# Segment attention with batch norm: unit weights for six segments' rows replaced by gathered weights, and 24 edge products a group by 16

## The chip, the cores and the metric

The kernel runs on one core of a Trainium2 chip. The metric is the device time of one execution in microseconds. Three timed executions of the kernel before gave 340.02, 339.72 and 338.75 us; the median is 339.72 us.

The engines as the profile names them: PE multiplies matrices (PEld is its loading of weights), DVE does vector work, ACT does activations and copies, POOL issues the indirect transfers (gathers and scatters) and some small vector work, SP issues the plain transfers. Each engine takes its instructions in order.

## The reference

There are 16384 tokens of 256 numbers (`feat`), and each has a segment number 0 to 7 (`bids`). The segment numbers are not sorted.

```python
q = feat @ Wq                 # 32 columns
k = feat @ Wk                 # 32 columns
v = feat @ Wv                 # 256 columns
starts = jnp.searchsorted(bids, jnp.arange(B))
pos = jnp.arange(N) - starts[bids]
pad = lambda x: jnp.zeros((B, LMAX, x.shape[-1])).at[bids, pos].set(x)   # LMAX 3072
mask = jnp.zeros((B, LMAX), bool).at[bids, pos].set(True)
scores = where(mask[:, None, :], qp @ kp^T, -1e9)
rp = softmax(scores) @ vp
t = rp[bids, pos] @ Wt
tn = (t - t.mean(axis=0)) / sqrt(t.var(axis=0) + EPS) * gamma + beta
return feat + relu(tn)
```

Because `bids` is not sorted, `pos` can be negative or beyond LMAX, and two tokens can be written to the same place of a segment. A token whose write stands is an *owner*; a token whose place was overwritten is a *loser*, and it reads the owner's row. A token whose position lies outside of the window reads the row at the window's near end: these are the *edge rows*, two for each segment, 16 in all. The mean and the variance go over all 16384 tokens, so every row of `t` counts as often as tokens read it.

## The kernel before, in words

**Owners.** The owners of segment `e` are gathered from `feat` into up to FT = 6 tiles of 128 rows, `xs[e*6 .. e*6+5]`. `list_ahead`, `list_sums` and `list_rows` work out the list of their tokens (`idx`) on DVE and PE, and `list_rows` issues three gathers on POOL for each half. There are 8 segments, so `xs` and the result `tk` have TT = 48 tiles. The losers make up LT = 3 tiles; their list is number NB = 8, their `feat` rows are in `xl` and their result rows in `tl`.

**Attention.** The loop over `e` works on segment `e` and prepares segment `e+1`. For each of six query tiles, `step(e, u)` calls `attend` (scores are exponentials in `pa` and `pb`, the product with the values in `vs`, a reciprocal) and `scale`, which writes `tk` and, after tiles 3 and 5, stores rows to the array `t_rows` in HBM through SP's queue. Between the steps stand the projections of the next segment, the lists of the segment after the next, and small jobs from the list `work` that `slot` takes one by one: `places`, `edges`, `fill_rows`, `rows`.

**Weights of rows.** `reads_r` has a column for each of the 48 tiles: how many tokens read each owner's row directly. `places().f` works out the counts by token and stores them to `reads_of` in HBM. For segments 0 to 5 (EARLY_B = 6), `list_ahead` sets the column to 1 where there is an owner and to 0 elsewhere, with one operation on DVE; the losers of these segments are added to the sums as rows of their own. For segments 6 and 7, `gather_reads` gathers the counts with six POOL gathers of one number a partition. After segment 6 the POOL queue gathers the losers' rows of segments 0 to 5 into `tl` (three gathers).

**Sums.** `square` squares a row tile on ACT into one of four buffers `sq`; `moments` adds the row and its square, each times its weight, into `acc` (two DVE operations). `past(e)` does `n` = 0, 0, 1, 1, 2, 2, 1, 1 pairs each time that it is called in segment `e`; in the last segment it has a branch of its own that does two pairs while loser tiles stand at the head of `lag` or more than one tile is waiting. The last segment takes its tiles in the order 0, 1, 4, 5, 2, 3, and after tile 3 what is left is done. Tile 1 of the last segment goes by PE (`by_row`) instead. At the end PE adds `acc` and the edge rows over the partitions into `sums`.

**Edge rows.** `ecat` holds the 16 edge rows, repeated so that partition `p` has row `p mod 16`: a gather from `t_rows` brings those of segments 0 to 6, and products with `sel` (written by POOL) add those of segment 7. `edge_of` holds for each token the code of its edge row, or a code of none. The codes are brought to all 128 partitions by 16 transfers through `eb`, and compared with `emod` (the partition number mod 16) into `hot`, a one-hot matrix in BF16.

**Statistics to output.** From `sums` DVE makes mean, variance, scale and shift (`ss`). Then it normalizes the edge rows (`ye`) and splits their positive part into three BF16 parts `y3[0..2]` whose sum is the value in full precision. The 16 output groups are of 1024 tokens each. For group `k`, `open_group` puts PAIRS[k] of its four pairs of `feat` tiles into PSUM by a product with the identity; 24 products (2 halves `u`, 3 parts, 4 row groups `r`, 16 partitions each) add the edge row of each token that reads one; DVE adds the other pairs, ACT copies those that PE opened, and SP stores 1 MB. From `k` = 3 on, DVE also normalizes one segment's owners after each group (`normal`, `normal_more`). POOL then scatters the owners' rows and the losers' rows over the stored groups, each segment after the groups that it needs (`finish` counts them).

**Order.** Waits are put in by the program class from what each operation reads and writes; each queue works in the order written. All operations are recorded by helpers, so the profile gives the helpers' lines: products L802, transposes L807, activations L812, copies L817 (ACT) and L818 (DVE), two-input operations L821, operations with a scalar L828 and L830, three-input operations L839 and L841, reciprocal L854, plain transfers L872, gathers L877, scatters L885 and L893, group loads L1703, group stores L1928.

Of the kernel before, what the change touches and what calls it, by code (L numbers as in the profile page):

```python
# [14 lines left out]
AF = mybir.ActivationFunctionType  # L15
ALU = mybir.AluOpType
# [884 lines left out]
def fast_path(nc, feat, bids, wq, wk, wv, wt, gamma, beta, out, bad):  # L901
# [74 lines left out]
    y3 = [at(f"y3{i}", [P, D], BF16, addr(acc) + 512 * i) for i in range(3)]  # L976

    pcol, pm, emod = new("pcol", [P, 1]), new("pm", [P, 1]), new("emod", [P, 1])
    ecol, rcol = new("ecol", [P, NB]), new("rcol", [P, FT])
    cbeg, cend, n_bc = new("cbeg", [P, NL]), new("cend", [P, NL]), new("n_bc", [P, NL])  # L980
    n_1 = new("n_1", [P, NL])
# [127 lines left out]
    pg.tt(sm[:], sm[:], sc_[:], ALU.subtract, eng="POOL")  # L1109
    pg.tt(sm[:], sm[:], sa[:], ALU.add, eng="POOL")  # L1110

    EARLY_B = NB - 2

    def zero_fill(e):
        rows = xs[:, e * FT : (e + 1) * FT, :].rearrange("p t d -> p (t d)")
        pg.copy("ACT", rows, zero[:].to_broadcast([P, FT * D]))
# [32 lines left out]
    def list_ahead(e):  # L1149
        T = FT if e < NB else LT  # L1150
        pg.ts(ge[:, 0, 0 : T * P], it16[:, 0 : T * P], cbeg[:, e : e + 1], ALU.is_ge)
        pg.ts(ge[:, 1, 0 : T * P], it16[:, 0 : T * P], cend[:, e : e + 1], ALU.is_ge, -1.0, ALU.mult)
        pg.ts(pad[:, 0:T], rcol[:, 0:T], n_bc[:, e : e + 1], ALU.is_ge, float(N), ALU.mult)
        if e < NB:
            m = slice(e * FT, e * FT + T)
            pg.ts(mask[:, m], rcol[:, 0:T], n_1[:, e : e + 1], ALU.is_ge, NEG, ALU.mult)
        if e < EARLY_B:
            pg.ts(reads_r[:, m], rcol[:, 0:T], n_bc[:, e : e + 1], ALU.is_lt)

    def list_sums(e, h, ps=None):  # L1160
        ps = nb() if ps is None else ps
# [132 lines left out]
    squared = []  # L1294

    def square(e, u):
        x = sq[turn[1] % (4 if e < NB - 1 else 3)]
        turn[1] += 1
        if e == NB:
            row, w = tl[:, u, :], ones[:, 0:1]  # L1300
        else:
            n = e * FT + u
            i = n - TT + FT - 2
            row, w = tk[:, n, :], rw[:, i : i + 1] if i in (0, 1) else reads_r[:, n : n + 1]
        pg.act(x[:], row, AF.Square)
        return row, w, x

    def own_of(e):
        pg.ts(own1[:], b_f[:], float(e), ALU.is_equal)
        pg.stt(own1[:], tok[:], st_lo[:, e : e + 1], own1[:], ALU.is_ge, ALU.mult)  # L1310
# [13 lines left out]

    pg.copy("POOL", bs_f[:], bs_i[:])
    def moments():
        row, w, s = squared.pop(0)
        pg.stt(acc[:, 0, :], row, w, acc[:, 0, :], ALU.mult, ALU.add)
        pg.stt(acc[:, 1, :], s[:], w, acc[:, 1, :], ALU.mult, ALU.add)

    cast_bids()
    pg.ts(own0[:], b_f[:], 0.0, ALU.is_equal, pm[:], ALU.mult)
# [118 lines left out]
    def edges():  # L1451
        def a():
            pg.ts(parts_i[:], pci[:], 2 * NB - 1, ALU.bitwise_and)
            pg.copy("DVE", emod[:], parts_i[:])
            pg.ts(g16[:], irow[0:1, 0:NG], float(GT * P), ALU.mult)
            pg.ts(at_g[:], g16[:], float(GT * P), ALU.add)
            lo = st_lo[0:1, :].unsqueeze(2).to_broadcast([1, NB, NG])
            hi = st_hi[0:1, :].unsqueeze(2).to_broadcast([1, NB, NG])
            pg.tt(over_g[:], hi, g16[:].unsqueeze(1).to_broadcast([1, NB, NG]), ALU.is_gt)
            pg.tt(over_h[:], lo, at_g[:].unsqueeze(1).to_broadcast([1, NB, NG]), ALU.is_lt)  # L1460
            pg.tt(over_g[:], over_g[:], over_h[:], ALU.mult)
            pg.red(need[:], over_g[:].rearrange("x e g -> x g e"), ALU.max)
            pg.scan(nth[:], ones[0:1, 0:NG], need[:])
# [171 lines left out]
    def fill_rows():  # L1635
        def zeros(x):
            f = x[:].rearrange("p t d -> p (t d)")
            pg.copy("ACT", f, zero[:].to_broadcast([P, f.shape[1]]))

        def a():  # L1640
            zeros(acc)
            pg.set("DVE", ridl[:], NB * FW)
            pg.set("DVE", reads_r[:, EARLY_B * FT : TT], 0.0)
            pg.tr32(gb[:].rearrange("p s i -> p (s i)"), graw[:].rearrange("p s i -> p (s i)"))

        def b():
# [10 lines left out]
    def by_row(w, row, x):  # L1657
        pg.mm(sums[:, 0:D], w[:], row, start=False, stop=False)
        pg.mm(sums[:, D : 2 * D], w[:], x[:], start=False, stop=False)

    work.extend(places())
# [12 lines left out]
    def past(e):  # L1674
        n = (0, 0, 1, 1, 2, 2, 1, 1)[e]
        if past_e[0] != e:
            past_e[:] = [e, 0]
        e_ = (e - 5) * FT + past_e[1]
        past_e[1] += 1
        if 0 <= e_ < NB:  # L1680
            load("DVE", ("td", e_), arm[0:1, e_ : e_ + 1], 2)
        if e == NB - 1:
            for _ in range(2 if lag and lag[0][0] == NB or len(lag) > 1 else 1):
                if squared:
                    moments()
                if lag:
                    squared.append(square(*lag.pop(0)))
            return
        for _ in range(n):
            if squared:  # L1690
                moments()
        for _ in range(n):
            if lag:
                squared.append(square(*lag.pop(0)))
# [12 lines left out]
    for e in range(NB):  # L1707
# [18 lines left out]
        if last:  # L1726
            for u in (0, 1, 4, 5, 2, 3):
                step(e, u)
                if u == 0:
                    for g in range(EARLY):  # L1730
                        load_group(g)
                    scores(e, 1, range(4))
                    late[0]()
                    late[1]()
                if u == 1:
                    scores(e, 1, range(4, 6))
                    late[2]()
                    pg.gather(ecat[:, 0, :], t_rows[0 : (NB - 1) * FW, :], eidx[:], (NB - 1) * FW)
                if u == 4:
                    late[3]()  # L1740
                if u == 0:
                    lag[:0] = [(NB, t) for t in range(LT)]
                if u == 5:
                    first = square(e, 1)
                    for g in range(EARLY, MID):
                        load_group(g)
                if u == 1:
                    pg.act(row_sum[:], ones[:], AF.Identity, scale=reads_r[:, e * FT + 1 : e * FT + 2])
                if u == 3:
                    any_ = hot[0 : 2 * NB, 0:2, :, :].rearrange("p k u x -> p (k u x)")  # L1750
                    pg.mm(sums[:], none[0 : 2 * NB, :], any_, start=True, stop=False)
                    by_row(row_sum, first[0], first[2])
                if u == 3:
                    while lag or squared:
                        if lag and len(squared) < 2:
                            squared.append(square(*lag.pop(0)))
                        else:
                            moments()
                else:
                    past(e)  # L1760
                if u == 2:
                    b_e = ps_s[0]
                    for u_ in (0, 4, 5, 1):
                        pg.mm(
                            b_e[:, 0:D], sel[:, u_, :], tk[:, e * FT + u_, :], start=(u_ == 0), stop=(u_ == 1),
                            pred=over4(e, u_),
                        )
                    pg.tt(ecat[:, 0, :], ecat[:, 0, :], b_e[:, 0:D], ALU.add)
                    pg.act(ecat[:, 1, :], ecat[:, 0, :], AF.Square)
        else:  # L1770
# [18 lines left out]
            step(e, 2, lambda: project(n, 1))  # L1789
            if busy:  # L1790
                list_part(e + 2, 1)
            past(e)
            slot(1 if busy else 2)
            if e + 3 < NB:
# [6 lines left out]
                own_of(e + 3)  # L1801
            if not busy:
                slot(2)
            if EARLY_B <= e + 1:
                gather_reads(e + 1)
            if e == 3:
                losers()[0]()
# [17 lines left out]
        pg.end_region()  # L1825
        if e == NB - 2:
            slot(99)
            for t in range(LT):
                pg.gather(tl[:, t, :], t_rows[0 : EARLY_B * FW, :], ridl[:, t : t + 1], EARLY_B * FW)
            pg.set("POOL", none[:], 0.0)  # L1830
    for e_ in range(NB + 1):
        load("POOL", ("g", e_), upto[0:1, e_ : e_ + 1], NG, 1)
# [50 lines left out]
    open_group(1)  # L1883
    pg.tt(ye[:], ecat[:, 0, :], scale, ALU.mult)
    pg.tt(ye[:], ye[:], shift, ALU.add)
    pg.ts(y3[0][:], ye[:], 0.0, ALU.max)
    pg.stt(yf[:], ye[:], 0.0, y3[0][:], ALU.max, ALU.subtract)
    pg.copy("DVE", y3[1][:], yf[:])
    pg.tt(y3[2][:], yf[:], y3[1][:], ALU.subtract)
    pg.tt(bad[:], b[:, 0:1], cnt_f[:, 0:1], ALU.add)  # L1890

    def normal(m, T, y=tk, x=xs):
# [40 lines left out]
    for k in range(NG):  # L1933
# [120 lines left out]
```

## Time and profile before

| what | value |
| --- | --- |
| median of three executions | 339.72 us |
| the profiled execution's own time | 340.02 us |
| its span (first to last instruction) | 335.6 us |
| outside of the span | 4.4 us |
| mean granted clock of PE | 0.865 |
| busy: PE, PEld, DVE, ACT, POOL | 258.8, 169.9, 238.0, 151.4, 135.4 us |
| `xs` gathers on POOL | 48, 1063 ns each |
| `reads_r` gathers on POOL | 12, 999 ns in the median |
| edge products `ps<-y,hot` | 384, in 16 groups of 24 |
| accumulations `acc` with `reads_r` | 45 and 45, 476 and 483 ns each |
| HBM read and written | 26.27 and 28.74 MB |

How to read it: in rows of single instructions or groups, the first number is the start in us from the beginning of the span, the second the duration in us (of several instructions of a kind, from the first to the last), then come engine, line, operation, the tile written and those read, and how many. In square brackets stands how long the engine was idle before it and what ended that. "remote" and "another core or an unknown queue" are put where the profile shows no instruction that ended at the time of the signal. In rows by windows, the columns are the stretch and its length, the busy time of PE, PEld, DVE, ACT and POOL with their counts, the granted clock of PE, the busy share of the DMA engines, and GB/s.

The execution has four stretches: lists, weights and first segment up to about 70 us; the middle segments up to about 217 us; the last segment with the statistics up to about 248 us; the output from there to the end.

### The profile page before, as it was taken

The numbers are of one execution on the slowest core, as the hardware profiler recorded it, in microseconds if no ns is written. First come the engines' busy times: TensorE is split into PE (matmuls) and PEld (weight loads), VectorE is DVE, ScalarE is ACT, GpSimd is POOL, SyncE is SP. The second block draws the span as 40 slices with busy tenths as digits, with TensorE's granted clock in tenths as the row PEclk, the third lists the DMA queues.
The fourth block names the chain that finished last, engine by engine and source line by source line (L and its number), as shares of the span: only waits on it lengthen the run. The fifth ranks groups of instructions, "written<-read, shape, count | busy, mean of one in ns | idle before, by whom it ended". The sixth has DMA issues, their size and how long they took to land.

```text
span 335.6 us, 4870 instructions
## 1 busy us (share of the span) xinstructions
PE 258.8 (77%) x1407; PEld 169.9 (51%) x1407; DVE 238.0 (71%) x765; ACT 151.4 (45%) x294; POOL 135.4 (40%) x143
## 2 busy tenths in 40 slices
PE   5699799998998999899999979295858966455100
PEld 2466556666666777677667856164423422122000
DVE  4835679996775759478759878445589999999202
ACT  3126968767755762656476377384310311110000
POOL 6434215060350160325003647742120647887750
PEclk9999989999999999999999999769585976555555
DMA  3101004151171033203001210399969999997933
GB/s 99 33 22 47 17 3 130 41 152 37 29 169 48 0 88 115 66 9 109 31 3 47 83 32 2 114 375 389 418 267 373 315 428 420 422 413 294 373 115 131
DMA packets 21533, 52.50 MB, mean 156 GB/s; under 512 B 5488, under 2 KB 14786, under 8 KB 17530
## 3 DMA queue, kind: packets, MB, share of 16 engines
q1 hardware_dynamic: 15674, 41.37, 32.4%
q0 software_dynamic: 5280, 10.18, 10.2%
q10 hardware_dynamic: 544, 0.52, 0.5%
q8 instruction: 16, 0.26, 0.3%
q14 instruction: 19, 0.16, 0.1%
HBM read 26.27 MB, written 28.74 MB: 164 GB/s over the span
## 4 chain that ended last, share of the span: by engine, by line
PE 45%; DVE 25%; ACT 9%; issue 6%; another core or an unknown queue 6%; POOL 3%; DMA 2%; POOLq 0%; DVEq 0%
PE ps L802 43%; DVE f L821 7%; DVE tk L821 5%; ACT pa L812 4%; ACT xT L812 2%; PE ps L807 2%; DMA ecat<-t_rows,eidx 2%; ACT vs L817 2%; DVE junk L828 1%; DVE k L818 1%; POOL sel L830 1%; DVE tk L1910 1%; DVE tk L1912 1%; DVE w L821 1%
## 5 line engine op out<-in xcount | busy, mean ns | idle before, releaser
L877 POOL DMA_INDIRECT xs<-in_r_feat,idx x48 | 51.0, 1063 | 118.9 <-DVE idx L841 70.3
L802 PE MATMUL ps<-vs,pa 128*128 128x257 f32 x312 | 80.7, 404 | 10.5 <-ACT tk L812 6.0
L802 PEld LDWEIGHTS ps<-vs,pa 128*128 128x128 f32 x312 | 59.1, 198 | 24.9 <-issue 10.3
L893 POOL DMA_INDIRECT out<-tk,idx x32 | 36.6, 1144 | 28.0 <-DVE f L821 15.8
L802 PE MATMUL ps<-wvt,xT 128*128 128x256 f32 x156 | 37.4, 386 | 0.7 <-ACT vs L817 0.7
L817 ACT COPY f<-ps 128x1024 f32<-128x1024 f32 (+1 forms) x12 | 10.0, 834 | 61.4 <-remote 40.2
L802 PE MATMUL ps<-y,hot 16*128 16x256 bf16 x384 | 20.1, 356 | 22.5 <-DVE f L821 14.5
L821 DVE TENSOR_TENSOR f<-f,ps 128x1024 f32<-128x1024 f32 (+3 forms) x17 | 26.2, 1561 | 14.9 <-remote 14.2
L802 PEld LDWEIGHTS ps<-wvt,xT 128*128 128x128 f32 x156 | 28.8, 190 | 11.0 <-ACT sq L812 2.3
L812 ACT ACTIVATE pa<-ps,mask 128x512 f32<-128x512 f32 x48 | 29.5, 687 | 10.2 <-PE ps L802 9.8
L802 PEld LDWEIGHTS ps<-y,hot 16*128 16x128 bf16 x384 | 11.0, 117 | 40.3 <-DVE f L821 21.3
L802 PE MATMUL ps<-f,ident 128*128 128x512 f32 x38 | 27.7, 854 | 1.6 <-DVE f L821 0.9
L854 DVE RECIPROCAL rdens<-ps 128x1 f32<-128x1 f32 x48 | 7.7, 160 | 27.3 <-PE ps L802 23.9
L817 ACT COPY vs<-ps 128x512 f32<-128x512 f32 x24 | 14.1, 589 | 27.1 <-PE ps L802 17.3
L812 ACT ACTIVATE xT<-ps,negx 128x512 f32<-128x512 f32 (+1 forms) x32 | 16.9, 581 | 19.4 <-PE ps L807 9.8
L818 DVE COPY k<-ps 32x128 f32<-32x128 f32 x48 | 14.1, 294 | 16.0 <-PE ps L802 13.3
L802 PE MATMUL ps<-xT,w 128*128 128x512 f32 (+1 forms) x48 | 22.0, 586 | 1.5 <-ACT xT L812 1.5
L812 ACT ACTIVATE q<-ps,cqk 96x512 f32<-96x512 f32 (+3 forms) x32 | 18.3, 573 | 10.3 <-PE ps L802 10.0
L841 DVE SCALAR_TENSOR_TENSOR acc<-tk,reads_r,acc 128x256 f32<-128x256 f32 x45 | 21.4, 476 | 2.0 <-issue 1.3
L841 DVE SCALAR_TENSOR_TENSOR acc<-sq,reads_r,acc 128x256 f32<-128x256 f32 x45 | 21.7, 483 | 0.0
L812 ACT ACTIVATE pb<-ps,mask 128x256 f32<-128x256 f32 x48 | 19.2, 475 | 4.1 <-PE ps L802 3.8
L802 PE MATMUL ps<-q,k 32*128 32x512 f32 (+1 forms) x124 | 20.0, 560 | 0.0
(264 smaller groups left out, 420.9 us busy)
## 6 DMA issues: line engine op xcount, KB each, us to landing
f<-in_r_feat SPq DMA_DIRECT2D x16, 1024.0 KB, 9.8
out<-f SPq DMA_DIRECT2D x15, 1024.0 KB
t_rows<-tk SPq DMA_DIRECT2D x8, 512.0 KB, 5.8
t_rows<-tk SPq DMA_DIRECT2D x8, 256.0 KB, 3.3
eb<-edge_of SPq DMA_DIRECT2D x16, 64.0 KB
out<-f SPq DMA_DIRECT2D x2, 512.0 KB, 3.4
xs<-in_r_feat,idx POOLq DMA_INDIRECT x48, 3.1
out<-tk,idx POOLq DMA_INDIRECT x39
```

Of the source, the lines that this page charges most:

```text
L802: "PE", lambda e: e.matmul(out, lhsT, rhs, start=start, stop=stop, skip_group_check=True),
L807: return self.op("PE", lambda e: e.transpose(out, in_, ident), [in_, ident], [out], pred=pred)
L812: "ACT", lambda e: e.activation(out, in_, func, bias=bias, scale=scale), [in_, *more], [out]
L817: return self.op("ACT", lambda e: e.copy(out, in_), [in_], [out])
L818: return self.op(eng, lambda e: e.tensor_copy(out, in_), [in_], [out])
L821: return self.op(eng, lambda e: e.tensor_tensor(out, a, b, op), [a, b], [out])
L828: lambda e: e.tensor_scalar(out, a, s1, s2, op0, op1, accum_out=accum)
L830: else e.tensor_scalar(out, a, s1, s2, op0, op1),
L841: else e.scalar_tensor_tensor(out, a, s, b, op0, op1),
L854: return self.op("DVE", lambda e: e.reciprocal(out, in_), [in_], [out])
L877: lambda e: e.indirect_dma_start(out=out, out_offset=None, in_=table, in_offset=bass.IndirectOffsetOnAxis(ap=ind, axis=0), bounds_check=n ...
L893: lambda e: e.indirect_dma_start(out=table, out_offset=bass.IndirectOffsetOnAxis(ap=ind, axis=0), in_=src, in_offset=None, bounds_check=n ...
```

## The change

- The six operations that set `reads_r` for segments 0 to 5 go; `gather_reads` is called for all eight segments, 36 more gathers on POOL: for segments 0 and 1 in segment 1 after the second half of the list of segment 3, for segments 2, 3 and 4 after the second half of the list in segments 2, 3 and 4, for segments 5, 6 and 7 after tile 4 of segments 4, 5 and 6. The counts then hold the losers of all segments.
- The three gathers into `tl` after segment 6 go, and so do the losers' three squares and six accumulations in the last segment. The gathers of all losers' rows before the statistics stay. `past` loses its branch for the last segment.
- The edge rows' split: `odd_` is 1 on partitions with bit 4 set, and `nodd` is -1 there. On even halves of 32 partitions the first BF16 part of the value stands, on odd halves the second, both in `y3[1]`; `y3[2]` has the third part on odd halves. `y3[0]` is used as an intermediate alone. The split has five DVE operations in place of four, and `edges().a` four small ones more.
- Each output group has 16 products of 32 partitions instead of 24 of 16 partitions. `hot` already has the code's one-hot in all 128 partitions.

```diff
     pcol, pm, emod = new("pcol", [P, 1]), new("pm", [P, 1]), new("emod", [P, 1])
+    odd_, nodd = new("odd_", [P, 1]), new("nodd", [P, 1])
...
-    EARLY_B = NB - 2
...
             pg.ts(mask[:, m], rcol[:, 0:T], n_1[:, e : e + 1], ALU.is_ge, NEG, ALU.mult)
-        if e < EARLY_B:
-            pg.ts(reads_r[:, m], rcol[:, 0:T], n_bc[:, e : e + 1], ALU.is_lt)
...
     def square(e, u):
+        n = e * FT + u
         x = sq[turn[1] % (4 if e < NB - 1 else 3)]
         turn[1] += 1
-        if e == NB:
-            row, w = tl[:, u, :], ones[:, 0:1]
-        else:
-            n = e * FT + u
-            i = n - TT + FT - 2
-            row, w = tk[:, n, :], rw[:, i : i + 1] if i in (0, 1) else reads_r[:, n : n + 1]
-        pg.act(x[:], row, AF.Square)
-        return row, w, x
-
+        pg.act(x[:], tk[:, n, :], AF.Square)
+        return n, x
...
     def moments():
-        row, w, s = squared.pop(0)
-        pg.stt(acc[:, 0, :], row, w, acc[:, 0, :], ALU.mult, ALU.add)
-        pg.stt(acc[:, 1, :], s[:], w, acc[:, 1, :], ALU.mult, ALU.add)
+        m, s = squared.pop(0)
+        x = m - TT + FT - 2
+        one = rw[:, x : x + 1] if x in (0, 1) else reads_r[:, m : m + 1]
+        pg.stt(acc[:, 0, :], tk[:, m, :], one, acc[:, 0, :], ALU.mult, ALU.add)
+        pg.stt(acc[:, 1, :], s[:], one, acc[:, 1, :], ALU.mult, ALU.add)
...
             pg.copy("DVE", emod[:], parts_i[:])
+            pg.ts(parts_i[:], pci[:], 2 * NB, ALU.bitwise_and)
+            pg.copy("DVE", odd_[:], parts_i[:])
+            pg.ts(odd_[:], odd_[:], 1.0 / (2 * NB), ALU.mult)
+            pg.ts(nodd[:], odd_[:], -1.0, ALU.mult)
...
-            pg.set("DVE", reads_r[:, EARLY_B * FT : TT], 0.0)
+            pg.set("DVE", reads_r[:], 0.0)
...
-        if e == NB - 1:
-            for _ in range(2 if lag and lag[0][0] == NB or len(lag) > 1 else 1):
-                if squared:
-                    moments()
-                if lag:
-                    squared.append(square(*lag.pop(0)))
-            return
...
-                if u == 0:
-                    lag[:0] = [(NB, t) for t in range(LT)]
...
-                    while lag or squared:
-                        if lag and len(squared) < 2:
-                            squared.append(square(*lag.pop(0)))
-                        else:
-                            moments()
+                    while lag:
+                        squared.append(square(*lag.pop(0)))
+                    while squared:
+                        moments()
...
             if busy:
                 list_part(e + 2, 1)
+            if e == 1:
+                gather_reads(0)
+            if 1 <= e < 5:
+                gather_reads(e)
...
-            if EARLY_B <= e + 1:
+            if e >= 4:
                 gather_reads(e + 1)
...
             slot(99)
-            for t in range(LT):
-                pg.gather(tl[:, t, :], t_rows[0 : EARLY_B * FW, :], ridl[:, t : t + 1], EARLY_B * FW)
             pg.set("POOL", none[:], 0.0)
...
-    pg.ts(y3[0][:], ye[:], 0.0, ALU.max)
-    pg.stt(yf[:], ye[:], 0.0, y3[0][:], ALU.max, ALU.subtract)
+    pg.ts(y3[0][:], ye[:], 0.0, ALU.max, nodd[:], ALU.mult)
+    pg.stt(yf[:], ye[:], 0.0, y3[0][:], ALU.max, ALU.add)
     pg.copy("DVE", y3[1][:], yf[:])
-    pg.tt(y3[2][:], yf[:], y3[1][:], ALU.subtract)
+    pg.tt(yf[:], yf[:], y3[1][:], ALU.subtract)
+    pg.ts(y3[2][:], yf[:], odd_[:], ALU.mult)
...
-            for part in range(3):
+            for part in (1, 2):
                 for r in range(4):
-                    s = slice(32 * r, 32 * r + 2 * NB)
+                    s = slice(32 * r, 32 * r + 32)
                     pg.mm(
                         bank[b0 + r][:, u * D : (u + 1) * D], hot[s, k, u, :], y3[part][s, :],
-                        start=(r < own_pairs and part == 0), stop=(part == 2),
+                        start=(r < own_pairs and part == 1), stop=(part == 2),
                     )
```

More of the change, by code (lines that the diff above doesn't have):

```diff
@@ L1655, in fast_path, with by_row @@
     sums = ps_s[1]
-    def by_row(w, row, x):
-        pg.mm(sums[:, 0:D], w[:], row, start=False, stop=False)
+    def by_row(w, m, x):
+        pg.mm(sums[:, 0:D], w[:], tk[:, m, :], start=False, stop=False)
         pg.mm(sums[:, D : 2 * D], w[:], x[:], start=False, stop=False)
@@ L1751, in fast_path @@
                     pg.mm(sums[:], none[0 : 2 * NB, :], any_, start=True, stop=False)
-                    by_row(row_sum, first[0], first[2])
+                    by_row(row_sum, *first)
                 if u == 3:
-                    while lag or squared:
-                        if lag and len(squared) < 2:
-                            squared.append(square(*lag.pop(0)))
-                        else:
-                            moments()
+                    while lag:
+                        squared.append(square(*lag.pop(0)))
+                    while squared:
+                        moments()
                 else:
```

## The prediction

> **What bounds the kernel now.** I read the stretches first (by windows: length, then busy PE, PEld, DVE, ACT and POOL, the granted clock, DMA share), then the chain that ended last, then the rows around each edit.
>
> ```profile
> 72.00:104.00 32.00, 29.91 (x146) 20.81 (x145) 24.41 (x93) 19.47 (x39) 8.93 (x8) 1.00 0.39 101
> 104.00:136.00 32.00, 30.79 (x162) 23.11 (x162) 21.33 (x90) 17.63 (x36) 8.37 (x8) 1.00 0.23 64
> 217.00:248.00 31.00, 23.30 (x89) 14.20 (x92) 18.20 (x68) 13.35 (x31) 9.08 (x11) 0.77 0.98 383
> 248.00:303.00 55.00, 37.08 (x328) 15.29 (x316) 53.73 (x58) 9.43 (x11) 30.68 (x26) 0.66 0.95 377
> 303.00:336.00 33.00, 6.40 (x74) 2.78 (x74) 11.70 (x8) 0.58 (x1) 16.67 (x17) 0.50 0.58 223
> ```
>
> The middle segments are bound by PE (29.91 and 30.79 of 32 us), and POOL has 23 us of every 32 to spare. From 248 to 303 DVE is busy for 53.73 of 55 us. After 303 no engine is: something is waited for. The chain says what:
>
> ```profile
> PE 45%; DVE 25%; ACT 9%; issue 6%; another core or an unknown queue 6%; POOL 3%; DMA 2%; POOLq 0%; DVEq 0%
> ...
> 72.47 2.57 another core or an unknown queue
> ...
> 112.90 21.69 PE ps L802 x114
> ...
> 211.14 4.34 another core or an unknown queue
> ...
> 227.72 6.84 DMA ecat<-t_rows,eidx
> ...
> 310.82 3.16 another core or an unknown queue
> ...
> 315.79 10.90 another core or an unknown queue
> ```
>
> Four waits, 20.97 us in all, have no recorded instruction at their end. In each, ACT or DVE waits for a signal of PE, whose recorded products ended long before. POOL issues indirect transfers in all four places; this is the reading on which my forecast rests. Rows of single instructions around it (start, duration, engine, what; in brackets the idle time before and what ended it):
>
> ```profile
> 211.88 1.14 POOL L877 DMA_INDIRECT reads_r<-reads_of,idx  x1 [0.30 <-issue]
> ...
> 215.46 0.59 ACT L817 COPY vs<-ps 128x512 f32<-128x512 f32 x1 [4.32 <-remote]
> ...
> 310.88 1.47 PE L802 MATMUL ps<-y,hot 16*128 16x256 bf16 x24 [0.73 <-DVE f L821]
> ...
> 323.56 0.98 POOL L893 DMA_INDIRECT out<-tl,idx  x1 [0.30 <-issue]
> 326.79 2.29 DVE L821 TENSOR_TENSOR f<-f,ps 128x2048 f32<-128x2048 f32 x1 [11.00 <-remote]
> ```
>
> The last group's products are recorded at 310.88, yet DVE may add only at 326.79, after POOL's last scatter at 323.56.
>
> **The change part by part.** The sum goes against the profiled execution: 335.6 us of span and 4.4 outside, 340.02 us, 0.30 above the median of the three runs.
>
> *Six weight operations removed.* Each `reads_r` operation holds DVE for 0.14 us (9.00 to 9.13). The first stands on the chain; at the second (19.85) the chain is PE, and later DVE has 7 to 11 us of slack in 32. Taken: -0.14; bounds -0.28 and 0.
>
> *36 gathers added.* One takes 1.00 us and 0.30 of issue on POOL, 46.8 us in all. Their places, against POOL's idle rows:
>
> ```profile
> 88.83 1.00 POOL L877 DMA_INDIRECT xs<-in_r_feat,idx  x1 [14.66 <-DVE idx L841]
> ...
> 116.58 1.00 POOL L877 DMA_INDIRECT xs<-in_r_feat,idx  x1 [19.15 <-DVE idx L841]
> ...
> 133.84 1.53 POOL L877 DMA_INDIRECT xl<-in_r_feat,idx  x1 [8.79 <-DVE idx L841]
> ...
> 179.46 1.06 POOL L877 DMA_INDIRECT xs<-in_r_feat,idx  x1 [20.41 <-DVE idx L841]
> ```
>
> Twelve in segment 1 need 15.6 us of a hole of 14.66 and push the next `xs` gathers by 1 us; these rows are used some 5 us after they land. Six need 7.8 us of the 19.15, six 7.8 of the 8.79, twelve 15.6 of the 20.41. So the queue holds them. The accumulations that will now wait for gathered counts come late enough: the first starts at 88.0, some 13 us after the first new gather can issue, and later segments have more. On DVE an accumulation takes 0.48 us beside a gather as without one (208.53 and 208.93, beside 207.77 and 209.07).
>
> The Trainium skill, page "SBUF — State Buffer", section "SBUF: two separate sides", speaks against this part: the port pair that DVE and GpSimd share is an exclusive lock held for a whole instruction. If the gathers' 1.00 us counted so, DVE could stand for up to an estimated 36 us in the middle; the accumulations of 0.48 us beside gathers do not show it.
>
> What remains is PE's late signal. Before 217 us the trace has 69 gathers (48 `xs`, 3 `xl`, 12 `reads_r`, 3 `ridl`, 3 `tl`) and 2.57 + 4.34 = 6.91 us of such waits on the chain: 0.10 us a gather. They stand where PE is the bound, so each ends on the path: ACT waits, and PE waits for ACT. Added less removed gathers are 33: 33 x 0.10 = 3.3 us. Bounds: 0, by the six `reads_r` gathers from 189.83, beside which the chain has no such wait; and 13.0, by the other six from 205.16, whose wait is 4.34, so 2.17 a set over the two, times six sets. I take the mean over all gathers, 3.3: the two sets of the same kind lie on both sides of it. What excludes a gain from adding them: nothing that they replace was on POOL.
>
> *Losers out of the sums.* Three `tl` gathers (POOL 213.33 to 216.92) go; they are counted above. Three pairs of accumulations go from 226.39 to 229.64; there DVE afterwards idles 3.23 us until the `ecat` gather lands, so their 2.4 us lengthen an idle time. What is late next is that landing: `sel` on POOL, its gather, 6.84 us. After it one pair of accumulations fewer stands (two of three). PE's next products are held to about 237.4 by its own work at half clock, and the last accumulation ends at 237.45: -0.1 taken; bounds -0.8 (a whole pair) and 0.
>
> *Four small operations in `edges().a`.* About 0.15 us each near 68 us, on DVE beside PE; cover is DVE's 7.6 us of slack. Taken 0; with the cover gone +0.6.
>
> *Split of the edge rows.* This is on the chain between statistics and output:
>
> ```profile
> 245.74 0.48 DVE L830 TENSOR_SCALAR y<-ye 128x256 bf16<-128x256 f32 x1
> 246.25 0.43 DVE L841 SCALAR_TENSOR_TENSOR yf<-ye,y 128x256 f32<-128x256 f32 x1
> 246.71 0.29 DVE L818 CAST y<-yf 128x256 bf16<-128x256 f32 x1
> 247.04 0.43 DVE L821 TENSOR_TENSOR y<-yf,y 128x256 bf16<-128x256 f32 x1
> ```
>
> One operation from FP32 to BF16 is added, 0.48 by the row of 245.74: +0.49 with its issue. PE, queued behind it, waits with the products of the third part. Of the first group's 24 products 16 stand behind that wait (0.70 us on the chain), afterwards 12: 0.70 x 12 / 16 = 0.53, so -0.17.
>
> *16 products instead of 24.* In groups 2 to 13 they stand beside DVE, the bound; taken 0. A group of 24 takes 0.83 us at full clock (260.99) and 1.47 at half (286.59). The Trainium skill, page "TensorE: Matmul & The Clock Gate", section "HAM oscillation", says that PE idle for more than about 3.4 us loses its clock; by the two rows 16 products at half clock would take 0.98 us, more than 24 at full, and the trace already grants 0.50 after 303. In the last two groups the waits of 3.16 and 10.90 could shrink with the number of products, by a third, 4.7 us; or stay, as the recorded products are 1.47 of it. I take 0: the wait ends with POOL's scatters, which the change leaves. A loss from fewer products on 32 partitions instead of 16 is bounded by 0.64 us, the step from full to half clock for one group on the path.
>
> Sum: -0.14 + 3.3 - 0.1 + 0 + 0.49 - 0.17 + 0 = +3.4 (3.38). 340.02 + 3.4 = 343.4 against the profiled execution, 343.1 against the median.
>
> **The rivals.**
>
> *No measurable change.* The 36 gathers cost nothing, as the six at 189.83. For it: the chain has no such wait between 75 and 211 us, with some 40 gathers in that time. Against it: the twelve in segment 1 stand as densely as those before 211. Sum 340.02 + 0.08 = 340.1, by the median 339.8. Half a per cent, 1.7 us, is about what a measurement of this kernel can tell from no change; so this holds while a gather costs less than 0.05 us.
>
> *Faster: the last group's signal comes earlier.* If PE's late signal is due to its many small products, a third of them fewer takes a third of 3.16 + 10.90 us: -4.7, to 335.4 with the +0.08, by the median 335.1. For it: the signals of groups 8 to 14 also come late by 1.5 to 3.8 us, only in this stage of small products. Against it: the waits at 72.47 and 211.14 have none. It decides when these two waits shrink by over 1.8 us while the gathers cost nothing. That the three `tl` gathers cause the 4.34 at 211.14 would give about as much; but the wait begins before the first of them (213.33).
>
> *The products do not matter at all* and only the weights part counts: this is the forecast itself without the 0.17, and not told apart by the time.
>
> *Dearer gathers.* At 0.20 us, with two waits like that at 211.14 among the four new runs of gathers, the time is 346.4 by the median.
>
> **How the numbers follow.** Slower by the gathers' late signals: 0.47 (of it 0.12 dearer than 345.5). No measurable change: 0.33. Faster by the end of the output: 0.20. The predicted time is the likeliest's, 343.1; its own range goes from 341.5 (0.05 a gather) to 347.1 (0.22). The range for 8 in 10 leaves out the lower part of the faster case and the dearest gathers: 337.5 to 346.5. Chances: faster by over 0.5% 0.20, within 0.5% 0.33, slower 0.47.
>
> **What would show it.** Right: new waits without a recorded releaser between 75 and 200 us, next to runs of `reads_r` gathers, 3 us in all; `tk` rows' accumulations still 0.48; the output stretch as long as now; an added 0.5 between the shift's application and the first product. Wrong: the middle segments unchanged in length (no change), or the add of the last group well before 326 (faster). The forecast errs if the releaserless waits follow something else than POOL's transfers, such as where PE's code lies, which the change shifts by its removed products; then their sum can fall anywhere from 0 to 21 us.

## The result: 5.7% slower on the chip of the measurement, and the profile after

The changed kernel took 358.0 us in the median of four executions (358.67, 361.78, 357.33, 356.52) against 339.36 us for the kernel before on the same chip: a ratio of 1.0566, with a 95% interval of 1.0479 to 1.0652. The profiled execution took 358.67 us, with a span of 354.0 us against 335.6.

The chain that ended last, on the page of the changed kernel, and those of its pieces that carry the loss (start, duration, what):

```profile
PE 43%; DVE 21%; another core or an unknown queue 9%; issue 9%; ACT 7%; POOL 5%; DMA 2%; POOLq 1%; DVEq 0%
```

```profile
71.25 6.75 another core or an unknown queue
78.02 0.59 ACT vs L817
78.61 10.63 another core or an unknown queue
...
143.45 7.18 another core or an unknown queue
...
189.76 7.58 another core or an unknown queue
...
237.06 3.18 issue
```

The waits without a recorded releaser now sum to 32.14 us, all before 217 us; before the change there were 6.91 us there, and 14.06 us in the last two groups, which are gone from the chain. The middle segments are no longer PE-bound where these waits stand. By windows (length, then busy PE, PEld, DVE, ACT and POOL, granted clock, DMA share):

```profile
72.00:104.00 32.00, 16.11 (x69) 10.85 (x68) 11.33 (x54) 9.99 (x20) 12.78 (x13) 0.73 0.15 41
104.00:136.00 32.00, 30.62 (x162) 22.86 (x161) 22.98 (x86) 20.11 (x40) 16.63 (x15) 1.00 0.21 61
...
303.00:354.00 51.00, 15.83 (x106) 5.15 (x106) 33.63 (x34) 3.78 (x5) 33.53 (x31) 0.50 0.80 316
```

From 72 to 104 us PE is busy for 16.11 us instead of 29.91, and so are DVE and ACT for half of what they were; DMA moves little. From 79.7 to 89.2 us, in the second wait, no engine but POOL is busy. Its rows and ACT's (start, duration, what; in brackets the idle time before):

```profile
73.08 1.00 POOL L877 DMA_INDIRECT reads_r<-reads_of,idx  x1 [0.30 <-issue]
...
78.02 0.59 ACT L817 COPY vs<-ps 128x512 f32<-128x512 f32 x1 [6.77 <-remote]
...
87.44 1.00 POOL L877 DMA_INDIRECT reads_r<-reads_of,idx  x1 [0.30 <-issue]
89.26 1.26 ACT L812 ACTIVATE pa<-ps,mask 128x512 f32<-128x512 f32 x2 [10.66 <-remote]
```

POOL issues 18 gathers without a pause (six of `xs`, twelve of `reads_r`, 65.3 to 88.4 us). ACT waits for two signals of PE, which come at 78.00 and 89.24 us; the second comes 0.8 us after the last gather has been issued. In the same stretch the register instructions by which SP reads the group order also took 0.69 us each for several of them (0.27, 0.15 and 0.02 us elsewhere). So it isn't PE's products that are slow.

Where the 18.4 us of span came from, by the first reciprocal of each segment (start of the segments), DVE's first addition to a group, and the end (differences from the unrounded times):

| stretch | before | after | difference |
| --- | --- | --- | --- |
| to the first segment | 37.2 | 36.0 | -1.2 |
| segment 0 | 21.9 | 22.0 | 0.0 |
| segment 1 | 19.7 | 35.2 | +15.5 |
| segments 2 and 3 | 59.2 | 65.6 | +6.4 |
| segments 4 and 5 | 60.8 | 66.5 | +5.7 |
| segment 6 | 22.3 | 18.5 | -3.8 |
| last segment and statistics | 27.1 | 27.1 | 0.0 |
| output to the end | 87.3 | 83.2 | -4.2 |

### The profile page after: what moved, and what is told of

Same layout as the page of the kernel before. It is cut to its first block, busy times and chain, and to the rows that moved or that the text cites. A ratio compares the mean times of both kernels' runs of the same rounds, so it can differ in the third digit from the quotient of the medians.

```text
span 354.0 us, 4676 instructions
## 1 busy us (share of the span) xinstructions
PE 255.9 (72%) x1279; PEld 167.0 (47%) x1279; DVE 236.8 (67%) x758; ACT 149.9 (42%) x291; POOL 168.0 (47%) x176
## 4 chain that ended last, share of the span: by engine, by line
PE 43%; DVE 21%; another core or an unknown queue 9%; issue 9%; ACT 7%; POOL 5%; DMA 2%; POOLq 1%; DVEq 0%
PE ps L802 41%; DVE tk L821 5%; DVE f L821 4%; POOL out L893 3%; ACT pa L812 2%; PE ps L807 2%; ACT xT L812 2%; DMA ecat<-t_rows,eidx 2%; ACT vs L817 2%; DVE junk L828 1%; DVE tk L1900 1%; DVE tk L1902 1%; DVE k L818 1%; POOL sel L830 1%
## 5 line engine op out<-in xcount | busy, mean ns | idle before, releaser
L877 POOL DMA_INDIRECT reads_r<-reads_of,idx x48 | 49.7, 1036 | 14.6 <-issue 14.6
L893 POOL DMA_INDIRECT out<-tk,idx x32 | 34.3, 1073 | 26.9 <-DVE tk L841 17.6
L802 PE MATMUL ps<-wvt,xT 128*128 128x256 f32 x156 | 39.0, 398 | 3.9 <-ACT vs L817 3.9
L802 PEld LDWEIGHTS ps<-wvt,xT 128*128 128x128 f32 x156 | 29.9, 197 | 14.8 <-ACT vs L817 5.9
L802 PE MATMUL ps<-y,hot 32*128 32x256 bf16 x256 | 15.1, 369 | 27.4 <-DVE f L821 19.6
L802 PEld LDWEIGHTS ps<-y,hot 32*128 32x128 bf16 x256 | 6.9, 116 | 44.0 <-DVE f L821 26.8
L802 PE MATMUL ps<-xT,w 128*128 128x512 f32 (+1 forms) x48 | 23.0, 606 | 5.2 <-ACT xT L812 5.2
L812 ACT ACTIVATE q<-ps,cqk 96x512 f32<-96x512 f32 (+3 forms) x32 | 18.4, 574 | 10.6 <-PE ps L802 10.3
```

What stands on the lines that cost most here:

```text
L802: "PE", lambda e: e.matmul(out, lhsT, rhs, start=start, stop=stop, skip_group_check=True),
L812: "ACT", lambda e: e.activation(out, in_, func, bias=bias, scale=scale), [in_, *more], [out]
L877: lambda e: e.indirect_dma_start(out=out, out_offset=None, in_=table, in_offset=bass.IndirectOffsetOnAxis(ap=ind, axis=0), bounds_check=n ...
L893: lambda e: e.indirect_dma_start(out=table, out_offset=bass.IndirectOffsetOnAxis(ap=ind, axis=0), in_=src, in_offset=None, bounds_check=n ...
```

## The experiments

Ratios are to the kernel before on the same chip. The runs fell on seven chips. On six of them (numbers 14, 12, 2, 9, 7 and 0) the kernel before takes 329.6 to 330.8 us, and no trace of these experiments has a late signal of PE; I call them chips with timely signals. Whether lateness belongs to the chip or to its condition at the time is not told apart: only chips 14 and 9 were met at more than one time. On chip 10 it takes 340.95 us, near the 339.36 on the chip of the first measurement, and the late signals are there; the number of that first chip is not recorded, so it may be the same one.

### Each half of the change alone

The first kernel is the kernel before with the split of the edge rows and the 16 products; the second is the changed kernel without them.

```diff
+    pg.ts(y3[0][:], ye[:], 0.0, ALU.max, nodd[:], ALU.mult)
+    pg.stt(yf[:], ye[:], 0.0, y3[0][:], ALU.max, ALU.add)
...
-            for part in range(3):
+            for part in (1, 2):
...
-                    s = slice(32 * r, 32 * r + 2 * NB)
+                    s = slice(32 * r, 32 * r + 32)
```

> The kernel before with the second half of the change alone: the edge rows' split and the 16 products a group; weights and losers stay as before. If the 36 gathers are the cause, this is the kernel before plus 0.3 us: 339 to 341 us, and the waits without a recorded releaser stay at 21 us in sum. If the products on 32 partitions are the cause (a later last group), it is 350 us or more. If fewer products shorten the wait for the last group by a third, it is about 335 us.

> The changed kernel with the edge rows' split and the 24 products of before: the weights' half of the change alone. If the 36 gathers are the cause: 357 to 359 us, with waits without a releaser of 5 to 11 us at the runs of gathers in segments 1, 3 and 5. If the two halves share the loss: between 345 and 352 us.

Chip 14: the products alone 330.24 us, ratio 0.9994 (0.9966 to 1.0023); the weights alone 328.04 us, ratio 0.9919 (0.9891 to 0.9948). The expected 358 us did not come, although the second kernel has the same runs of gathers. The products are worth nothing that can be measured there; the weights' half is a gain.

### The gathers spread, and a run of gathers by itself

In the first, each gather waits for the reciprocal of the step behind which it stands; in the second and third the kernel before gets 12 or 36 more gathers, into a tile that nobody reads (the edit of the second is shown; the third has them at the 36 places of the changed kernel).

```diff
+            [ind, reads_of], [dst], dma=True, after=(anchor[0],),
...
+        for r in ((), (), (1,), (2, 3), (4, 5), (6,), (7,), ())[e]:
+            gather_read(r, u)
```

```diff
+            if e == 1:
+                for m in range(12):
+                    pg.gather(spare[:, m : m + 1], reads_of, idx[:, m : m + 1], N)
```

> The changed kernel with the same 48 gathers of weights, but one or two behind each step of a segment, each held back until that step's reciprocal, so that POOL pauses between them. If each gather costs the same wherever it stands (the theory of number): 358 us as the changed kernel. If only a long run of gathers without a pause holds up PE's signals (the theory of runs): 339 to 344 us, and no wait without a releaser over 3 us between 60 and 240 us.

> The kernel before, plus twelve gathers of the counts into an unused tile, in one run behind the second half of segment 3's list in segment 1, where the changed kernel has its first twelve; nobody reads them. If the run itself holds up PE's signals: 353 to 356 us (the changed kernel's waits of 6.75 and 10.63 us there, less the 2.57 that stand there before). If it is that the sums wait for the gathered counts: 339 to 341 us. By 0.10 us a gather, as I forecast: 341 us.

> The kernel before plus 36 gathers of the counts into an unused tile, at the 36 places of the changed kernel; nobody reads them. This is the price of the added gathers by themselves. Where PE's signals come in time it is 0 (within 0.5% of the kernel before); where they come late it is the whole of the loss, 15 to 20 us. By my forecast of 0.10 us a gather: 3.6 us.

> The kernel before plus 36 unread gathers at the changed kernel's places, one look for the same case. Late signals: 355 to 360 us if the gathers by themselves are the whole of the loss. Timely signals: 331 us.

Spread, chip 14: 328.59 us, 0.9944 (0.9908 to 0.998). Twelve more: 330.26 us, 0.9983 (0.9956 to 1.0009). Thirty-six more, chip 12: 331.83 us, 1.0020 (0.9990 to 1.0050), and on chip 2, in single executions, 333.4 against 329.94. So on chip 12 36 gathers are worth 0.7 us, -0.3 to 1.7 by the interval, and their spread gains nothing over the changed kernel unspread (0.9871 to 0.9896, below). Both the theory of runs and that of number foretold a loss here; neither can hold for the kernel alone. POOL issued 30 gathers without a pause there, and no signal came late.

The Trainium skill, page "SBUF — State Buffer", section "SBUF: two separate sides", says that of GpSimd and certain operations of DVE the one that gets the shared port pair first holds it for its whole instruction, and the other blocks. If the gathers of 1.00 us counted so, 36 of them could hold up DVE. They cost 0.7 us, and DVE is busy for 237.5 us beside them, against 238.0 in the profile of the kernel before: the measurement speaks against reading these gathers so.

### The changed kernel again

> The changed kernel itself once more, beside the kernel before on the same chip. The four kernels run so far lie within 1% of the kernel before, and their traces have no wait without a releaser, though three of them have the runs of gathers. If the slowdown belongs to the kernel: 5 to 6% above the kernel before, with waits without a releaser of 5 to 11 us in segments 1, 3 and 5. If it belongs to the condition of the chip in the first measurement: 0.5 to 1% below the kernel before and no such wait.

> The changed kernel for the third time, to see whether the late signals of PE come back. On the two chips of the runs so far there are none, and the changed kernel is 1.1% faster than the kernel before; in the first measurement they cost it 20 us. If they belong to some chips: either about 328 us with no wait without a releaser, or about 358 us with those of segments 1, 3 and 5.

> The changed kernel beside it. Late signals: 356 to 360 us as in the first measurement. Timely signals: 326 to 328 us.

Chip 12 (five executions): 327.81 us, ratio 0.9891 (0.9830 to 0.9952). Chip 14 (two): 326.36 us, 0.9871 (0.9820 to 0.9922). Chip 0 (two): 326.91 us, 0.9896 (0.9837 to 0.9955). On three chips the same kernel that lost 5.7% gains 1.0 to 1.3%. The profile of chip 14 spans 321.4 us and that of the first measurement 354.0, 32.6 us more for the same program; the waits without a releaser in the latter sum to 32.14 us. So they account for all but 0.5 us of the difference. The chain of the trace from chip 14 has no piece without a releaser, and the stretch that was half idle is full:

```profile
by line: PE ps L802 43.9%; issue 8.5%; DVE tk L821 5.8%; DVE f L821 4.7%; POOL out L893 3.6%; ACT pa L812 3.0%; PE ps L807 2.2%; DMA ecat<-t_rows,eidx 2.1%; ACT xT L812 1.9%; DVE junk L828 1.7%; ACT vs L817 1.6%; DVE k L818 1.4%; DVE tk L19
```

```profile
72.00:104.00 32.00, 29.65 (x148) 21.41 (x147) 24.05 (x91) 19.13 (x38) 24.99 (x24) 1.00 0.37 92
104.00:136.00 32.00, 30.62 (x163) 22.96 (x162) 21.32 (x89) 17.80 (x35) 16.91 (x17) 1.00 0.25 69
```

POOL is busy for 24.99 of 32 us with gathers there, and PE loses nothing.

### What the gain is: three gathers ahead of the edge rows

The changed kernel gets the three gathers of the losers' rows behind segment 6 back, unread.

```diff
             slot(99)
+            for t in range(LT):
+                pg.gather(tl[:, t, :], t_rows[0 : (NB - 2) * FW, :], ridl[:, t : t + 1], (NB - 2) * FW)
             pg.set("POOL", none[:], 0.0)
```

> The changed kernel with the three gathers into tl behind segment 6 put back; nobody reads them, as the rows are gathered again later. In the runs with timely signals the first sel on POOL starts 0.97 us after the last segment's first reciprocal without them and 4.14 us with them. If these three gathers on the way to the edge rows are what the change gains, this kernel loses the gain: 0 to 0.3% from the kernel before, some 3 us above the changed kernel, with sel at 4.1 us. If the gain is the losers' accumulations or the products, it stays 1% below. Should the signals come late: 358 to 362 us.

Chip 9: 332.28 us, ratio 1.0058 (1.0032 to 1.0085). The gain is lost, and 0.6% more, which was not expected. The changed kernel itself did not run on this chip, so ratios are compared here. POOL's rows say how. The kernel before with 36 more gathers:

```profile
213.86 1.00 POOL L877 DMA_INDIRECT tl<-t_rows,ridl  x1 [0.30 <-issue]
214.87 0.22 POOL L860 MEMSET none<- 128x128 bf16 x1
215.18 4.90 POOL L830 TENSOR_SCALAR sel<-edge,rcol 128x128 f32<-128x128 f32 x6
```

and the changed kernel on chip 14:

```profile
209.33 1.08 POOL L877 DMA_INDIRECT reads_r<-reads_of,idx  x1 [0.30 <-issue]
210.41 0.22 POOL L860 MEMSET none<- 128x128 bf16 x1
211.63 5.48 POOL L830 TENSOR_SCALAR sel<-edge,rcol 128x128 f32<-128x128 f32 x6 [1.00 <-DVE edge L821]
```

With the three gathers `sel` starts as soon as POOL is free, 4.14 us after the last segment's first reciprocal (4.15 in this experiment); without them it waits 1.00 us for `edge`, and starts 0.97 us after it. POOL's queue is ahead of `sel`, `sel` ahead of the gather of `ecat`, and this one ahead of the statistics. In the profile of the kernel before, on the chip with late signals, `sel` started at 222.20, 5.06 us after POOL was free, since `edge` came late; there the three gathers were covered by the late signal.

The other experiments on chips with timely signals agree. Where `sel` starts 4.14 us after the reciprocal, the ratios lie between 0.9983 and 1.0058; where it starts after 0.97 or 0.98, between 0.9864 and 0.9944, apart from the last experiment below, which delays the output. How much of the loss on chip 9 the 3.2 us account for stays open: the profile's output also took 87.0 us, against 83.3 for the changed kernel on chip 14.

### Once more on chips as they came, until the late signals returned

The spread kernel of above:

> The changed kernel with its gathers of weights held back to one or two behind each step, as before. Where the signals come late in the changed kernel: 340 to 345 us if the length of a run of gathers decides, 358 us if their number does. Where they come in time: 328 to 330 us, no gain from spreading.

> The changed kernel with its gathers held back to one or two behind each step, one look for the case that PE's signals come late again (the kernel before then at 339 us instead of 330). Late signals: 340 to 345 us if the length of a run decides, 358 us if the number of gathers decides. Timely signals: 328 us.

> The changed kernel with its gathers held back to one or two behind each step, one look on whichever chip comes. If PE's signals come late here (the kernel before at 339 us): 340 to 345 us if the length of a run of gathers decides, 358 us if their number does. If they come in time (the kernel before at 330 us): 327 to 329 us.

> As the run before it, on whichever chip comes. Late signals (the kernel before at 339 us): 340 to 345 us by runs, 358 us by number. Timely signals: 327 to 330 us.

On chips 14, 2 and 7: 327.96 against 330.48 us (the recorded ratio is 0.9864, with a wide interval of 0.9764 to 0.9965), 328.77 against 329.94 and 329.86 against 330.78, without late signals. The last fell on chip 10: 347.1 us against 340.95 us, single executions. That is outside what either theory foretold for late signals (340 to 345, and 358). Its chain has the late signals:

```profile
72.44 6.16 another core or an unknown queue
79.21 3.75 another core or an unknown queue
...
134.36 6.99 another core or an unknown queue
...
179.67 1.48 another core or an unknown queue
...
324.09 8.17 another core or an unknown queue
```

In the middle they sum to 18.4 us, between the kernel before (6.9) and the changed kernel (32.1), both on the chip of the first measurement. The changed kernel did not run on chip 10, so it is not shown that spreading saves anything there. The spreading was incomplete: next to the gathers of the lists POOL still has runs of 10 to 12 at 65.7 to 81.1, 98.6 to 112.4, 126.4 to 139.3 and 163.6 to 179.6 us, and three of these four are where the middle waits stand. Between 55 and 260 us it also has eighteen runs of one to six gathers, and beside these stands no late signal. In the changed kernel it is alike: late signals at runs of 18, 9, 15 and 9 (beside the last, DVE waits for 2.25 us at 237.6, within the 3.18 us that the chain calls issue), none at those of 3 and 6; but the run of 12 from 104.6 to 121.6 us and the one of 9 from 212.4 had none either. The kernel before has one exception: its wait of 2.57 us at 72.47 stands beside a run of six (66.5 to 74.2). So a run of nine or more goes with every other late signal of the middle, but does not always bring one.

### Shorter runs

The 48 gathers go two at a time behind steps without list gathers.

```diff
+        if e == 1 and u >= 3 or 2 <= e < 6 and u in (0, 3, 4, 5) or e == 6:
+            for _ in range(2):
+                if to_read:
+                    gather_read(*to_read.pop(0))
```

> The changed kernel with its 48 gathers of weights two at a time, behind the steps that have no list gathers beside them, so that no run is longer than about 6. On the chip with late signals the first spread kernel lost 6 us to the kernel before, all its late signals beside runs of 10 to 12. Late signals (the kernel before at 340 us): at or below the kernel before, 335 to 341 us, if runs of about ten or more are needed; 347 us or more if the number counts. Timely signals: 327 to 330 us.

> The kernel with the gathers two at a time, beside the changed kernel on one chip. Late signals: at or below the kernel before (335 to 341 us), 17 us or more under the changed kernel, if the length of a run decides. Timely signals: 328 to 332 us, up to 4 us above the changed kernel, for what POOL's waits between the pairs cost.

Both fell on chips with timely signals: 331.9 us against 329.6 (chip 9, one execution each), and 330.54 us, 1.0013 (0.9981 to 1.0046), on chip 0, where the changed kernel took 326.91 us. The deciding case was not met. What the runs do show is the price of holding gathers back: more of them come in the last segments, `sel` again starts 4.14 us after the last segment's first reciprocal, and 3.6 us are lost to the changed kernel.

### An earlier start of the scatters

The experiments point to POOL's scatters, of which the last 38 of 42 follow each other without a pause, as the end on chips with timely signals (on chip 14 they end at 313.2 us, DVE's last addition at 304.6). The changed kernel with each segment's rows normalized one group earlier:

```diff
-        if 3 <= k < 3 + NB:
-            e = k - 3
+        if 2 <= k < 2 + NB:
+            e = k - 2
```

> The changed kernel, with each segment's owner rows normalized one output group earlier (from the third group on instead of the fourth), so that POOL's scatters begin earlier. On the chips with timely signals POOL's unbroken chain of 38 scatters ends the kernel some 10 us after DVE's last addition; if its start decides, the end comes 4 us earlier, about 324 us. If the stores of the groups that a segment needs decide, no change: 328 us.

Chip 14: 330.31 us, ratio 0.9987 (0.9966 to 1.0009), 4 us above the changed kernel on the same chip. The first scatters start at 251.6 instead of 250.6 us, and the last ends at 317.2 instead of 313.2: POOL waits for SP's stores of groups (4.36 us ahead of 262.30, 1.60 ahead of 276.77); that the rows' work delays the groups is the likely reason, not a shown one. No version found here beats both kernels on both kinds of chips.

## Why the prediction was wrong

The time, 358.0 us, lies far above the range of 337.5 to 346.5. The step that failed is the price of the added gathers. The sign was right, but by luck of the chip: on three others the same change is faster. Point by point:

- **36 gathers, 33 x 0.10 = 3.3 us: this term failed, by its size.** The kind is as forecast: waits without a releaser for PE's signals, next to runs of `reads_r` gathers, on PE's path. On the measurement's chip they grew by 32.14 - 6.91 = 25.2 us, 0.76 us for each of the 33. The unit was wrong: a mean over all 69 gathers spreads the waits over runs that had none, while the change lengthened runs to 9, 15 and 18. Even the upper bound of 13.0 took a set of six as unit and was too low, and the range did not reach to it. Compared across chips, the kernel before took 9 us more on the first chip (339.4 against some 330.4), the changed one 31 (358.0 against some 327.0): if the gain of 3.4 us that the timely chips show is also in it on the first chip, late signals became dearer by 22 us, of which 18.6 are left.
- **"Each ends on the path": wrong for the wait at 72.47.** From the first reciprocal of segment 1 to that of segment 3 the kernel before takes 46.71 us with this wait of 2.57 us; the products alone on chip 14, with the same work in these segments and no such wait, take 46.56. It cost 0.15 us: where the signal is in time, ACT waits for PE one step later instead, by 1.96 us. So the 6.91 us from which the price was taken were not all a cost.
- **What the prediction did not hold for possible:** on chips with timely signals the same term is close to nothing, 0.02 us a gather on chip 12, within the 0.05 of the rival of no measurable change. The condition under which the forecast was made, late signals, does not occur on them.
- **The three `tl` gathers, counted only as gathers: wrong where the signals are timely.** They stand in POOL's queue ahead of `sel`; without them `sel` starts 3.2 us earlier, and their return turned 0.987 to 0.990 into 1.0058. I saw `sel` as what is late next, but gave POOL's queue ahead of it no price, as the profile of before shows POOL free 5.06 us earlier. That slack was made by a late signal.
- **The last two groups, taken 0 because the wait ends with POOL's scatters: wrong.** In the changed kernel the last addition starts at 339.25 after 4.22 us of idling instead of 11.00, and the scatters go on to 345.8. The output became 4.2 us shorter, near the rival's 4.7. Of this 2.8 us are the late addition: in the other eighteen profiles the span ends 8.25 us after POOL's last scatter, in the kernel before 11.05 after it, and there the end waits for the store behind the last addition. That the smaller number of products is what made the signal less late is not shown: on chips with timely signals the products alone are worth nothing (0.9994).
- **Split of the edge rows, +0.49 - 0.17 = +0.32: right.** From the first `ye` to DVE's first addition 3.84 us against 3.43, +0.41.
- **One pair of accumulations fewer, -0.1: right within its bounds.** From the addition to `ecat` to the transposition of the sums it is 6.75 us in both, so 0.0.
- **Removed weight operations, -0.14; four small operations, 0:** the first segment starts 1.2 us earlier and segment 0 is the same. The terms are not tested by this: in the profiles of the experiments the first segment starts anywhere from 33.2 to 37.4 us.

ACT around the wait at 72.47, in the kernel before and then in the products alone on chip 14:

```profile
75.07 0.58 ACT L817 COPY vs<-ps 128x512 f32<-128x512 f32 x1 [2.60 <-remote]
75.55 1.27 ACT L812 ACTIVATE pa<-ps,mask 128x512 f32<-128x512 f32 x2
...
72.18 0.59 ACT L817 COPY vs<-ps 128x512 f32<-128x512 f32 x1 [0.34 <-PE ps L802]
74.73 1.27 ACT L812 ACTIVATE pa<-ps,mask 128x512 f32<-128x512 f32 x2 [1.96 <-PE ps L802]
```

The split of the changed kernel and its last two additions:

```profile
267.01 0.42 DVE L821 TENSOR_TENSOR ye<-ecat,ss 128x256 f32<-128x256 f32 x1
...
269.57 0.61 DVE L830 TENSOR_SCALAR y<-yf,odd__109 128x256 bf16<-128x256 f32 x1
...
270.85 1.82 DVE L821 TENSOR_TENSOR f<-f,ps 128x1024 f32<-128x1024 f32 x2 [0.61 <-PE ps L802]
...
333.27 1.75 DVE L821 TENSOR_TENSOR f<-f,ps 128x1536 f32<-128x1536 f32 x1
339.25 2.29 DVE L821 TENSOR_TENSOR f<-f,ps 128x2048 f32<-128x2048 f32 x1 [4.22 <-remote]
```

Open is what makes PE's signals late on the chip of the first measurement and on chip 10, and not on six others, and whether the length of a run is its cause there or only goes with it; even that the added gathers lengthened the waits rests on where these stand, as no run on such a chip had the gathers alone. It is not the place of the code by itself, which the prediction named as a way to err: the same program has the waits on one chip and not on three others. The late sequencer steps of SP in the same stretch show that it isn't PE alone.

## What to carry to other kernels

A wait without a recorded releaser may belong to the chip, or to its condition at the time, and not to the kernel: before a forecast rests on it, look whether a second chip has it, and if that can't be had, give both cases their price. Price a recurring stall by the stretch beside which it stands (here a long run of gathers), not by a mean over all instructions of the kind, and ask of each wait whether anything behind it was held up. And when such a stall is in the profile, the slack that stands behind it is not cover: take the stall away in thought, and see which queue is then the last.

## What the runs showed of the hardware

The same program takes 330 us on six chips and 340 us elsewhere (339.36 on the first measurement's chip, 340.95 on chip 10), with the mean granted clock at 0.84 to 0.89 in all. For the changed kernel, 354.0 us of span against 321.4, the difference is that of the late signals between engines (32.14 us), which stand beside long runs of POOL's indirect transfers. Such a run costs next to nothing where the signals are timely: 36 more gathers cost 0.7 us, and POOL is busy for 24.99 of 32 us beside a PE busy for 29.65.
